# The third product of a finished block takes the identity and layer 2's root matrix along: rows of h and their root part from one product, in a two-layer relational graph network on one Trainium2 core

## The chip, the cores and the metric

The kernel runs on 1 core of one Trainium2 chip, as one program. The metric is the device time of one execution in microseconds (us). Before the change it is 3677.3 us, the median of 3 runs (3677.16, 3677.3 and 3686.43). Five engines run side by side and meet at semaphores: PE (matrix products; PEld is its loading of weights), DVE (vector operations), ACT (activations and copies), POOL (here it issues the gathers) and SP (it issues most of the other transfers).

## The reference

Two relational graph layers with a residual and a layer norm, over N = 12500 nodes, E = 200000 edges sorted by their target `dst`, C = 128 features and 10 relations; an edge's relation is the argmax of 10 of its 42 attributes.

```
def _rgcn_layer(x, src, dst, edge_type, w_rel, root, bias):
    N = x.shape[0]
    seg = dst * NUM_REL + edge_type
    xs = x[src]
    sums = jax.ops.segment_sum(xs, seg, num_segments=N * NUM_REL)
    cnt = jax.ops.segment_sum(jnp.ones(seg.shape, x.dtype), seg, num_segments=N * NUM_REL)
    mean = (sums / jnp.maximum(cnt, 1.0)[:, None]).reshape(N, NUM_REL, -1)
    return jnp.einsum('nrd,rdo->no', mean, w_rel) + x @ root + bias
...
edge_type = jnp.argmax(msg[:, NODE_EMB_DIM:-NODE_EMB_DIM], axis=1).astype(jnp.int32)
h = jax.nn.relu(_rgcn_layer(x, src, dst, edge_type, w_rel1, root1, b1))
return _rgcn_layer(h, src, dst, edge_type, w_rel2, root2, b2)
...
x = _layernorm(x + _L0_gnn_ref(...), axis=-1)
```

All of it is float32.

## The kernel before

**Tiles and blocks.** The edges lie in 1563 tiles of 128. Layer 1 walks over them in parts of `QB` = 4 tiles; this is the unit `u` of all times in the code, and `v` is half of it. For each tile POOL gathers the 128 source rows from memory (`gathered`, L835), DVE makes a matrix of weights by target (`oh`, L842), PE multiplies the two (`zp`, L1079), and two parts later DVE adds the result to `cc`, the sums by relation and node of a moving window (L868). PE, DVE, ACT, POOL and SP each work through their instructions in the order in which the program was written; a list `todo` of due times, in tiles, says behind which tile a step of other work is written.

The nodes lie in 52 blocks, most of them of 256 nodes (two halves of 128). Once the last edge of a block's nodes is summed, `finish(k, t)` writes the block's end into the stream of tiles:

- ten products of the sums with layer 1's weights and one of x's columns `fT` with root 1 (L828, L830) into PSUM, and the relu on ACT: `a`, the block's h as columns (L747). This is at once.
- Half a part later, for blocks 0 to `K1` = 43, `rows_out`: PE turns `a` into rows with two transposes (L953). Another half a part later, `rows_kept`: ACT copies them to `hb`, whose other half holds the rows of x (L960), and SP stores x and h side by side into `XH` (256 KB, L700). Later tiles whose source lies in a finished block gather these 256 columns: the x half serves layer 1, the h half layer 2's sums, so that an edge is gathered once for both layers.
- After one part, SP stores the block's layer-2 sums SD (1.28 MB, L803) and loads the next block's x.
- After two parts SP stores `a` to `hT` (128 KB, L965).
- After 2, 3, ... 7 parts, one step each of `projected_rows`: a 128-row half of h times layer 2's weights of relations 0 to 3, 4 to 7 (512 columns) and 8 to 9 (256 columns), into the one PSUM buffer `yb` (L936). Each step first writes the copy of the step before (`kept_rows`): ACT moves `yb` to one of two buffers `ys` (L942), and SP stores that to `YD` (L944). YD holds h times each relation's weights, and layer 2 gathers its rows for the edges whose source wasn't finished in time.
- After 5 and 6 parts the next block's x is turned on PE and copied by ACT (L998, L1005), and ACT clears parts of `cc` (L797).

**Layer 2** gathers from YD, with products `zy` and `zq` (L1620), sums on DVE into `acc2` (L1650), and for the SD sums products with layer 2's weights (L1533, L1540). A block's columns of `acc2` begin with `begun` (L1510, L1511): PE multiplies the loaded `hT` by root 2 into PSUM, and ACT adds the bias and writes `acc2`; three loads of `hT` are under way at a time. Its end turns `acc2` into rows on PE (L1552); DVE adds the rows of x, which are loaded for it, and norms them (L775 to L785).

In the trace's names `w` is a layer's weights, `root` its root matrix, `g` a gathered tile, `pf` a general PSUM tile with two buffers.

Of the kernel before, what the change touches and what calls it, by code (L numbers as in the profile page):

```python
# [9 lines left out]
F32 = mybir.dt.float32  # L10
# [10 lines left out]
P = 128  # L21
# [49 lines left out]
def rgcn_resnorm_kernel(ctx: ExitStack, tc: tile.TileContext, x, src, dst, attr, w_rel1, root1, b1,  # L71
# [152 lines left out]
    hT = dram.tile([C, N], F32, name="hT")  # L224
    XH = dram.tile([2 * N, 2 * C], F32, name="XH")
# [27 lines left out]
    ident = const.tile([P, P], F32, name="ident")  # L253
# [247 lines left out]
    def weights_in():  # L501
        for l, (wr, ro, bi) in enumerate(((w_rel1, root1, b1), (w_rel2, root2, b2))):
            t = const.tile([P, NREL, C], F32, name=f"w{l}")
            later(nc.sync.dma_start(t, wr.rearrange("r d o -> d r o")))
            wsb.append(t)
            t = const.tile([P, C], F32, name=f"root{l}")
# [198 lines left out]
    hbs = {}  # L705

    def rows_in(k):

        if home[0] is prep:
            if k == NBLK - 1:  # L710
                xb = fin.tile([P, 1, C], F32, name="xbe")
            else:
                hbs[k] = prep.tile([P, 2, 2 * C], F32, name=f"hb{k % 2}")
                xb = hbs[k][:, :, :C]
# [193 lines left out]
    def layer_1():  # L908
# [6 lines left out]
        def finish(k, t):  # L915
# [16 lines left out]
            def projected_rows(b, h, r):  # L932
                kept_rows()
                m = min(HB, NREL - r) * C
                yb = yb_ if u else next_of("zp", fixed)
                nc.tensor.matmul(yb[:h, :m], fin_a[k][:, b * P:b * P + h], wsb[1][:, r:r + m // C, :], start=True, stop=True)  # L936
                unkept.append(lambda: projected_kept(yb, b, h, r))

            def projected_kept(yb, b, h, r):
                ys = next_of("ys", staged)  # L940
                m = min(HB, NREL - r) * C
                nc.scalar.activation(ys[:h, :m], yb[:h, :m], AF.Copy)  # L942
                n0 = block(k)[0] + 1 + b * P
                nc.sync.dma_start(by_node[n0:n0 + h, r * C:r * C + m], ys[:h, :m])  # L944
# [3 lines left out]
            def rows_out(_):  # L948
                a = fin_a[k]
                pr = ps_f.tile([P, 4, C], F32, name="pf")  # L950
                n0, n, subs = block(k)
                for i, h in subs:
                    nc.tensor.transpose(pr[:h, i, :], a[:, i * P:i * P + h], ident)  # L953
                po.append(pr)

            def rows_kept(_):
                pr = po.pop()
                hb = hbs.pop(k)
                for p, s in spans(k):
                    nc.scalar.activation(hb[:p, s, C:], pr[:p, s], AF.Copy)  # L960
                rows_dma(hb, XH[N:], k, True)

            def features_kept(_):
                n0, n, _ = block(k)
                nc.sync.dma_start(hT[:, n0:n0 + n], fin_a[k][:, :n])  # L965

# [861 lines left out]
```

## Time and profile before

| what | value |
|---|---|
| median of 3 runs | 3677.3 us |
| the profiled execution, its time | 3672.03 us |
| the profiled execution, its span | 3670.2 us, 37654 instructions |
| mean granted TensorE clock | 0.753 |
| gathers of layer 1 from XH: x1386 | 1309.9 us of POOL, 945 ns each |
| gathers of layer 2's remaining edges, lists E and B: x177 and x678 | 168.2 and 640.3 us of POOL |
| projections of finished blocks, L936: x576 | 354.9 us of PE, 383.3 us idle before them |
| root products of layer 2, L1510: x102 | 39.2 us of PE, 65.3 us idle before them |

The table is read like this: "busy" is what an engine's instructions of a line took in all, "idle before" how long the engine stood just ahead of them, and the trace names what ended that. A 128-row product of float32 is recorded as two instructions. A tile of 128 edges is one gather.

### The profile page before, as it was taken

How to read it: one execution, taken by the hardware profiler on the slowest of the kernel's cores; microseconds unless marked ns; L12 is line 12 of the kernel's file. 1: busy time of each engine (PE TensorE's matmuls, PEld its weight loads, DVE VectorE, ACT ScalarE, POOL GpSimd, SP SyncE). 2: the span in 40 equal slices, each digit the busy share in tenths (PEclk: the TensorE clock that was granted, in tenths of full speed). 3: DMA queues.
4: the chain of work that ended last, by engine and by line, in shares of the span. 5: the costliest groups of instructions: out<-in, count | busy, mean ns of one | idle time of the engine just before them, and what ended most of it. 6: DMA issues, size and time to landing. Idle time of an engine off the chain costs nothing. (4 is left out here: it accounts for less than half of the span.)

```text
span 3670.2 us, 37654 instructions
## 1 busy us (share of the span) xinstructions
PE 2319.0 (63%) x10645; PEld 1779.5 (48%) x10645; DVE 1991.3 (54%) x6410; ACT 511.8 (14%) x799; POOL 2287.4 (62%) x2430
## 2 busy tenths in 40 slices
PE   1557676767676767677666767653566666566444
PEld 0445565555555555565555655543534343333333
DVE  4646476767575757565655656358644232332332
ACT  1111111212121212121212121110000000000000
POOL 5663666666666666666666666556666666666665
PEclk7677787888887888878888878765667777677555
DMA  4553555455555555555555555542334443443222
GB/s 121 159 164 94 187 157 186 151 167 159 177 174 159 189 158 190 158 192 159 190 156 188 159 159 156 147 111 55 105 112 139 129 153 123 148 152 116 61 57 52
DMA packets 345316, 529.25 MB, mean 144 GB/s; under 512 B 55520, under 2 KB 225723, under 8 KB 345100
## 3 DMA queue, kind: packets, MB, share of 16 engines
q0 software_dynamic: 99552, 249.45, 23.9%
q1 hardware_dynamic: 218105, 264.48, 21.7%
q10 hardware_dynamic: 27443, 12.82, 1.2%
q8 instruction: 89, 1.46, 0.2%
q14 instruction: 127, 1.04, 0.1%
HBM read 372.75 MB, written 160.19 MB: 145 GB/s over the span
## 5 line engine op out<-in xcount | busy, mean ns | idle before, releaser
L835 POOL DMA_INDIRECT g<-XH,idxE x1386 | 1309.9, 945 | 769.7 <-issue 368.6
L1079 PEld LDWEIGHTS zp<-oh,g 128*128 128x128 f32 x5898 | 918.4, 234 | 396.5 <-DVE cc L868 180.1
L1079 PE MATMUL zp<-oh,g 128*128 128x120 f32 x5898 | 957.0, 320 | 228.6 <-DVE cc L868 132.3
L868 DVE TENSOR_TENSOR cc<-cc,zp 128x240 f32 (+1 forms) x1563 | 606.5, 388 | 816.1 <-remote 354.1
L835 POOL DMA_INDIRECT g<-YD,idxB x678 | 640.3, 944 | 342.4 <-issue 190.7
L936 PE MATMUL yb<-w,a 128*128 128x512 f32 (+1 forms) x576 | 354.9, 706 | 383.3 <-ACT ys L942 229.0
L842 DVE TENSOR_SCALAR oh<-bank,keyE,wE 128x120 f32<-128x120 f32 x1563 | 517.3, 393 | 0.0
L1620 PEld LDWEIGHTS zy<-oh,g 128*128 128x128 f32 x1168 | 244.8, 275 | 317.9 <-DVE cc L1650 119.1
L1620 PE MATMUL zy<-oh,g 128*128 128x12 f32 (+30 forms) x1168 | 258.4, 347 | 206.5 <-DVE cc L1650 114.6
L942 ACT ACTIVATE ys<-yb 128x512 f32<-128x512 f32 (+2 forms) x291 | 152.8, 525 | 1384.8 <-remote 612.0
L1533 PE MATMUL alone<-cc,w 128*128 128x512 f32 (+1 forms) x440 | 305.3, 782 | 31.6 <-issue 16.9
L936 PEld LDWEIGHTS yb<-w,a 128*128 128x128 f32 x576 | 111.0, 240 | 413.7 <-ACT ys L942 255.9
L828 PE MATMUL pf<-cc,w 128*128 128x256 f32 (+2 forms) x1040 | 254.9, 401 | 25.7 <-issue 13.4
L835 POOL DMA_INDIRECT g<-in_x_dram,idxE x177 | 167.3, 945 | 138.2 <-PE zp L1079 60.0
L828 PEld LDWEIGHTS pf<-cc,w 128*128 128x128 f32 x1040 | 208.4, 215 | 63.9 <-issue 26.0
L835 POOL DMA_INDIRECT g<-YD,idxE x177 | 168.2, 951 | 110.8 <-issue 62.7
L775 DVE TENSOR_TENSOR cc<-pf,x 128x256 f32<-128x256 f32 (+2 forms) x52 | 21.2, 409 | 358.9 <-remote 219.9
L797 ACT ACTIVATE cc<-zero 128x1280 f32<-128x1280 f32 x170 | 214.6, 1262 | 0.0
L1620 PEld LDWEIGHTS zq<-oh,g 128*128 128x128 f32 x542 | 110.8, 253 | 151.2 <-DMA g<-YD,idxB 74.0
L842 DVE TENSOR_SCALAR oh<-columns,keyB,wB 128x45 f32<-128x45 f32 (+35 forms) x678 | 176.8, 335 | 0.0
L1620 PE MATMUL zq<-oh,g 128*128 128x45 f32 (+33 forms) x542 | 122.9, 341 | 84.3 <-DMA g<-YD,idxB 59.5
L1650 DVE TENSOR_TENSOR cc<-cc,zy 128x12 f32 (+24 forms) x306 | 59.0, 193 | 142.6 <-remote 61.0
(265 smaller groups left out, 1528.4 us busy)
## 6 DMA issues: line engine op xcount, KB each, us to landing
cc<-SD SPq DMA_DIRECT2D x21, 2560.0 KB
SD<-cc SPq DMA_DIRECT2D x41, 1280.0 KB
YD<-ys SPq DMA_DIRECT2D x194, 256.0 KB
m<-in_edge_attr_dram SPq DMA_DIRECT2D x48, 672.0 KB
g<-XH,idxE POOLq DMA_INDIRECT x1386
YD<-ys SPq DMA_DIRECT2D x97, 128.0 KB
XH<-hb SPq DMA_DIRECT2D x44, 256.0 KB
g<-YD,idxB POOLq DMA_INDIRECT x678
```

Source lines behind the costliest of these rows:

```text
L775: nc.vector.tensor_tensor(v[:p, s], pr[:p, s], xb[:p, s], op=ALU.add)
L797: nc.scalar.activation(cc[:, l, h * H:(h + 1) * H, o:o + n], zero[:, None, :n].to_broadcast([P, H, n]), AF.Copy)
L828: nc.tensor.matmul(po[:, :n], wsb[l][:, r, :], sums[:, r], start=(r == 0), stop=(w is None and r == NREL - 1))
L835: nc.gpsimd.indirect_dma_start(out=g[:, j * C:(j + n) * C], out_offset=None, in_=table, in_offset=bass.IndirectOffsetOnAxis(ap=idx, axis=0))
L842: nc.vector.tensor_scalar(oh[:, j * m:(j + 1) * m], cols[:, :m], keys[:, j:j + 1], weights[:, j:j + 1], op0=ALU.is_equal, op1=ALU.mult)
L868: nc.vector.tensor_tensor(s, s, z, op=ALU.add)
L936: nc.tensor.matmul(yb[:h, :m], fin_a[k][:, b * P:b * P + h], wsb[1][:, r:r + m // C, :], start=True, stop=True)
L942: nc.scalar.activation(ys[:h, :m], yb[:h, :m], AF.Copy)
L1079: nc.tensor.matmul(zp[:, o + l * KW:o + (l + 1) * KW], g[:, (slot[j] + l) * C:(slot[j] + l + 1) * C], oh[:, j * KW:(j + 1) * KW], start=Tr ...
L1533: nc.tensor.matmul(po[:, :n], wsb[1][:, r, :], sds[j][:, r, :n], start=(r == 0), stop=(r == NREL - 1))
L1620: nc.tensor.matmul(zp[:, o:o + w], g[:, at * C:(at + 1) * C], oh[:, j * w:(j + 1) * w], start=not second or j == 0, stop=not second or j = ...
L1650: nc.vector.tensor_tensor(s, s, zps[q][:, j * w:(j + 1) * w], op=ALU.add)
```

## The change

Layer 2's weights, its root matrix and the identity now lie side by side in one tile of 12 matrices, `w2`: relations 0 to 9, root, identity. The product of a half with "relations 8 and 9" is widened:

- For blocks 0 to 43 it takes 512 columns: relations 8 and 9, root, identity. It so gives the half's part of YD, the root part of layer 2, and the rows of h. It is now the first of a block's projections, for both halves at once (`rows_out`, half a part after the finish), one half into `yb`, the other into a `pf` tile. The transposes go. `rows_kept` copies both halves to the two `ys`; SP stores the rows of h to XH (64 KB a half) and the part of YD. The x half of XH is copied by SP from x in memory at the finish.
- One part later DVE adds the rows of x to the root part in `ys`, and SP stores that to a new array `XR` (`root_kept`, 64 KB a half). A `ys` buffer is taken again only when this is done.
- Four projections of 512 columns remain, after 2 to 5 parts.
- For blocks from 44 on the third product takes 384 columns (relations 8 and 9, root), and the root part goes to XR too.
- `hT` is neither stored nor loaded; `begun` only writes the bias to `acc2`; the end of layer 2 loads its rows from XR in place of x.

The core of the diff:

```
+    XR = dram.tile([N, C], F32, name="XR")
...
-    ident = const.tile([P, P], F32, name="ident")
+    w2 = const.tile([P, NREL + 2, C], F32, name="w1")
+    root = w2[:, NREL, :]
+    ident = w2[:, NREL + 1, :]
...
+            def projected_rows(t, b, h, r, yb=None):
+                if yb is None:
+                    kept_rows(t)
+                    yb = yb_ if u else next_of("zp", fixed)
+                m = width(r)
+                nc.tensor.matmul(yb[:h, :m], fin_a[k][:, b * P:b * P + h], w2[:, r:r + m // C, :], start=True, stop=True)
+                unkept.append(lambda t: projected_kept(t, yb, b, h, r))
+
+            def width(r):
+                return (HB if r + HB <= NREL or k <= K1 else NREL + 1 - r) * C
+
+            def projected_kept(t, yb, b, h, r):
+                if len(unrooted) == len(staged) or unrooted and unrooted[0][0] == turn_of_["ys"] - len(staged):
+                    unrooted.pop(0)[1]()
                 ys = next_of("ys", staged)
+                m = width(r)
                 nc.scalar.activation(ys[:h, :m], yb[:h, :m], AF.Copy)
+                n0 = block(k)[0] + b * P
+                q = min(HB, NREL - r) * C
+                if k <= K1 and m > q:
+                    nc.sync.dma_start(XH[N + n0:N + n0 + h, C:], ys[:h, q + C:q + 2 * C])
+                nc.sync.dma_start(by_node[n0 + 1:n0 + 1 + h, r * C:r * C + q], ys[:h, :q])
+                if m > q:
+                    one = turn_of_["ys"] - 1, lambda: root_kept(ys, n0, b, h, q)
+                    unrooted.append(one)
+                    todo.at(min(END, t + u), lambda _: one in unrooted and (unrooted.remove(one), one[1]()))
...
+            def root_kept(ys, n0, b, h, q):
+                nc.vector.tensor_tensor(ys[:h, q:q + C], ys[:h, q:q + C], xbs[k][:h, b, :], op=ALU.add)
+                nc.sync.dma_start(XR[n0:n0 + h, :], ys[:h, q:q + C])
+
+            def rows_out(t):
+                kept_rows(t)
+                for (b, h), yb in zip(block(k)[2], (yb_, ps_f.tile([P, YB], F32, name="pf"))):
+                    projected_rows(t, b, h, last, yb)
+
+            def rows_kept(t):
+                while unkept:
+                    unkept.pop(0)(t)
...
+            if k <= K1:
                 n0, n, _ = block(k)
-                nc.sync.dma_start(hT[:, n0:n0 + n], fin_a[k][:, :n])
+                nc.sync.dma_start(XH[N + n0:N + n0 + n, :C], x[n0:n0 + n, :])
...
         def begun(j):
-            po = ps_f.tile([P, YB], F32, name="pf")
-            nc.tensor.matmul(po[:, :n], rsb[1], fTs.pop(k)[:, :n], start=True, stop=True)
-            nc.scalar.activation(acc2[:, n0:n0 + n], po[:, :n], AF.Identity, bias=bsb[1])
-            features_in_turn(j + 3)
+            n0, n, _ = block(begin[j])
+            nc.scalar.activation(acc2[:, n0:n0 + n], zero[:, :n], AF.Identity, bias=bsb[1])
...
-                rows_dma(xbs[finals[j]], x, finals[j], False)
+                rows_dma(xbs[finals[j]], XR, finals[j], False)
```

PE, in layer 1, behind the finish of one block (the names: `zp` the products of edge tiles, `yb` and `pf` PSUM, `a` the block's h as columns, `w_391` layer 2's weights). Before:

```order
L1079 MATMUL zp_407<-oh_92,g_88 128x120 x2
L953 MATMUL pf<-ident,a 128x128 x2
L1079 MATMUL zp_408<-oh_92,g_88 128x120 x2
L1079 MATMUL zp_409<-oh_93,g_88 128x120 x2
L1079 MATMUL zp_410<-oh_93,g_88 128x120 x2
L936 MATMUL yb<-w_391,a 128x512
L1079 MATMUL zp_407<-oh_94,g_89 128x120 x2
L1079 MATMUL zp_408<-oh_94,g_89 128x120 x2
L936 MATMUL yb<-w_391,a 128x512
L1079 MATMUL zp_409<-oh_95,g_89 128x120 x2
L297 MATMUL pf<-ident,s_f 128x128
L1079 MATMUL zp_410<-oh_95,g_89 128x120 x2
```

And the same block in the changed kernel (`w_114` is the tile of 12 matrices, so that the last row, a small turn of edge data with the identity, names it too):

```order
L1087 MATMUL zp_406<-oh_93,g_89 128x120 x2
L937 MATMUL yb<-w_114,a 128x512
L937 MATMUL pf<-w_114,a 128x512
L1087 MATMUL zp_407<-oh_93,g_89 128x120 x2
L1087 MATMUL zp_408<-oh_94,g_89 128x120 x2
L1087 MATMUL zp_409<-oh_94,g_89 128x120 x2
L937 MATMUL yb<-w_114,a 128x512
L1087 MATMUL zp_406<-oh_95,g_90 128x120 x2
L1087 MATMUL zp_407<-oh_95,g_90 128x120 x2
L937 MATMUL yb<-w_114,a 128x512
L1087 MATMUL zp_408<-oh_96,g_90 128x120 x2
L300 MATMUL pf<-w_114,s_f 128x128
```

The two transposes have become two products of 512 columns, the second of them into `pf`; the next projection stands where the first stood before, and the 256-column one behind the second of 512 is gone: the fourth 512-column projection now stands one step earlier.

SP, for one block in the middle of layer 1, with what each row waits for beside being next in line (a DMAHW semaphore is one of eight that SP's transfers use in turn). Before, all ten transfers of a block:

```order
L700 DMA XH<-hb_7834 128x2x256 [waits DMAHW1_49,Activation_49]
L803 DMA SD<-cc 1280x1x256 [waits DMAHW2_49]
L700 DMA hb_8190<-in_x_dram 128x2x128 [waits DMAHW3_49,PE_49]
L965 DMA hT<-a 128x256 [waits DMAHW4_49]
L944 DMA YD<-ys_99 128x512 [waits DMAHW5_49,Activation_49]
L944 DMA YD<-ys_100 128x512 [waits Activation_49]
L944 DMA YD<-ys_99 128x256 [waits DMAHW7_49,Activation_49]
L944 DMA YD<-ys_100 128x512 [waits DMAHW0_49,Activation_49]
L944 DMA YD<-ys_99 128x512 [waits DMAHW1_49,Activation_49]
L944 DMA YD<-ys_100 128x256 [waits DMAHW2_49,Activation_49]
```

After, the first twelve of the thirteen transfers of a block (the last, another store to YD, is left out):

```order
L978 DMA XH<-in_x_dram 256x128 [waits DMAHW3_49]
L952 DMA XH<-ys_100 128x128 [waits DMAHW4_49,Activation_49]
L953 DMA YD<-ys_100 128x256 [waits DMAHW5_49]
L952 DMA XH<-ys_101 128x128 [waits DMAHW6_49,Activation_49]
L953 DMA YD<-ys_101 128x256 [waits DMAHW7_49]
L803 DMA SD<-cc 1280x1x256 [waits DMAHW0_49,DVE_49]
L703 DMA xb_8564<-in_x_dram 128x2x128 [waits DMAHW1_49,PE_49]
L963 DMA XR<-ys_100 128x128 [waits DMAHW2_49,DVE_49]
L963 DMA XR<-ys_101 128x128 [waits DMAHW3_49,DVE_49]
L953 DMA YD<-ys_100 128x512 [waits DMAHW4_49,Activation_49]
L953 DMA YD<-ys_101 128x512 [waits DMAHW5_49,Activation_49]
L953 DMA YD<-ys_100 128x512 [waits DMAHW6_49,Activation_49]
```

The one store of x and h has become a copy of x at the front and two stores of h's rows, each with a store to YD behind it; the store of `hT` is gone; the two XR stores stand behind the store of the sums and the load of the next x, and ahead of the first of the four remaining stores to YD.

PE, at one place in layer 2 (`alone` are the products of the stored sums, `zy` those of gathered edges). Before:

```order
L1533 MATMUL alone<-cc,w_391 128x512
L1620 MATMUL zy_15679<-oh_93,g_86 128x85 x2
L1533 MATMUL alone<-cc,w_391 128x512
L1384 MATMUL pf<-ident,keyb 38x1
L1510 MATMUL pf<-cc,root_393 128x256 x2
L1620 MATMUL zy_15680<-oh_94,g_86 128x89
L1533 MATMUL alone<-cc,w_391 128x512
L1620 MATMUL zy_15680<-oh_94,g_86 128x89 x2
```

After:

```order
L1529 MATMUL alone<-cc,w_114 128x512
L1614 MATMUL zy_15778<-oh_94,g_87 128x85 x2
L1529 MATMUL alone<-cc,w_114 128x512
L1392 MATMUL pf<-w_114,keyb 38x1
L1614 MATMUL zy_15779<-oh_95,g_87 128x89
L1529 MATMUL alone<-cc,w_114 128x512
L1614 MATMUL zy_15779<-oh_95,g_87 128x89 x2
L1529 MATMUL alone<-cc,w_114 128x512
```

The pair of root products is gone from between the edge products, and nothing stands in its place.

More of the change, by code (lines that the diff above doesn't have):

```diff
@@ L704, in rgcn_resnorm_kernel @@
     home = [prep]
-    hbs = {}
     def rows_in(k):
@@ L964, in features_kept @@
+            last = NREL // HB * HB
+            groups = [(b, h, r) for b, h in block(k)[2] for r in range(0, NREL, HB) if k > K1 or r < last]
+            if k <= K1:
                 n0, n, _ = block(k)
-                nc.sync.dma_start(hT[:, n0:n0 + n], fin_a[k][:, :n])
-            groups = [(b, h, r) for b, h in block(k)[2] for r in range(0, NREL, HB)]
-            if k <= K1:
+                nc.sync.dma_start(XH[N + n0:N + n0 + n, :C], x[n0:n0 + n, :])
                 todo.at(t + v, rows_out)
@@ L1558, in layer_2 @@
             nc.sync.dma_start(rowP[:, c * CT:(c + 1) * CT], b_i[c:c + 1, :])
-        for j in range(3):
-            features_in_turn(j)
         for j in range(3):
```

56 lines of the change are left out of this document (10 added, 46 removed).

## The prediction

> **What bounds the kernel now.** I read the page's totals first, then two long stretches of the busy-time windows, then the waits and the groups by shape inside the first of them.
>
> ```profile
> span 3670.2 us, 37654 instructions
> PE 2319.0 (63%) x10645; PEld 1779.5 (48%) x10645; DVE 1991.3 (54%) x6410; ACT 511.8 (14%) x799; POOL 2287.4 (62%) x2430
> ...
> core 0: us, PE busy (x) PEld busy (x) DVE busy (x) ACT busy (x) POOL busy (x), PEclk, DMA share, GB/s
> 500.00:2300.00 1800.00, 1259.57 (x6514) 1021.22 (x6512) 1142.80 (x3369) 361.67 (x497) 1143.15 (x1210) 0.82 0.54 169
> 2700.00:3450.00 750.00, 467.99 (x1643) 292.86 (x1641) 251.60 (x1090) 26.25 (x72) 489.91 (x519) 0.73 0.42 133
> ```
>
> No engine is full anywhere. The first stretch is the steady part of layer 1; it holds 38 finished blocks (38 stores of the sums, and 152 copies of 512 columns at four a block), so a block takes 1800/38 = 47.4 us. The second is the late part of layer 2. POOL issues gathers of 0.945 us, and between two that wait for nothing stand 0.30 us (the timeline below: 1533.34, 1534.59, 1535.84). So its own pitch is 1.25 us, and 1210 gathers would need 1512 of the 1800 us; 288 us, or 7.6 us a block, are POOL standing. In layer 2, 519 gathers need 649 of 750 us, and about 101 us are standing.
>
> What POOL stands for in layer 1 is PE, which frees the gathered tiles late, and what PE stands for is this:
>
> ```profile
> POOL g L835 <- issue: 323.0, 1051, 0.8
> POOL g L835 <- remote: 170.6, 81, 3.1
> POOL g L835 <- PE zp L1079: 136.0, 58, 7.6
> POOL g L835 <- DMA XH<-hb: 0.6, 2, 0.3
> ...
> PE yb L936 <- ACT ys L942: 184.7, 57, 8.6
> PE yb L936 <- issue: 97.6, 32, 7.9
> ...
> L936 PE MATMUL yb<-w,a 128*128 128x512 f32 x304 | 221.4, 819 | 245.9 <-ACT ys L942 142.9 <-issue 73.1 <-DMA g<-XH,idxE 29.9
> L936 PE MATMUL yb<-w,a 128*128 128x256 f32 x152 | 61.3, 491 | 66.7 <-ACT ys L942 41.9 <-issue 24.5
> L953 PE MATMUL pf<-ident,a 128*128 128x128 f32 x72 | 16.9, 321 | 43.4 <-ACT a L747 34.7 <-DMA g<-XH,idxE 8.0 <-issue 0.7
> ```
>
> The reader sees one dominant wait on PE: a projection step (L936) into the single buffer `yb` waits until ACT has copied the step before it to `ys`. The two L936 rows carry 245.9 + 66.7 = 312.6 us of idle, 8.2 us a block over six steps. This is close to the 7.6 us that POOL stands, so I take layer 1 as a loop limited by PE with its waits for ACT, with POOL little behind. PE waits for gathered data little (29.9 + 8.0 us in 38 blocks): it has a stock of gathers.
>
> One passage of the timeline shows such a wait:
>
> ```profile
> 1530.74 0.38 ACT L960 ACTIVATE hb<-pf 128x256 f32<-128x256 f32 x1 [1.84 <-PE zp L1079]
> 1531.15 0.37 SPq L700 DMA_DIRECT2D XH<-hb  x1
> 1531.61 0.52 SPq L803 DMA_DIRECT2D SD<-cc  x1
> 1532.49 1.03 PE L936 MATMUL yb<-w,a 128*128 128x512 f32 x2
> 1533.34 0.95 POOL L835 DMA_INDIRECT g<-XH,idxE  x1 [0.30 <-issue]
> 1534.59 0.95 POOL L835 DMA_INDIRECT g<-XH,idxE  x1 [0.30 <-issue]
> 1535.84 0.95 POOL L835 DMA_INDIRECT g<-XH,idxE  x1 [0.30 <-issue]
> 1541.16 0.60 ACT L942 ACTIVATE ys<-yb 128x512 f32<-128x512 f32 x1 [8.88 <-issue]
> 1541.81 1.22 PE L936 MATMUL yb<-w,a 128*128 128x512 f32 x1 [6.15 <-ACT ys L942]
> ...
> q1 hardware_dynamic: 1584, 1.58, 86.7%
> ```
>
> The first `yb` is done at 1533.5, its copy starts only at 1541.16, and PE stands 6.15 us. Between them lies the 1.28 MB store SD; in the six microseconds from 1532 on, SP's queue q1 moved 1.58 MB, so SD alone takes about 1.31/1.58 x 6 = 5.0 us (an estimate from that row).
>
> **The change, part by part, layer 1.** 44 blocks (0 to 43) take the new form.
>
> 1. Two 256-column steps a block go, with their waits. Busy 61.3/38 = 1.61 us, idle 66.7/38 = 1.76 us: -3.37 us. The steps left are the four 512-column ones, and I keep their waits as they are.
> 2. The transposes of L953 go: 16.9 us for 36 recorded blocks, -0.47 us. The wait ahead of them (43.4 us) is for the relu `a`; the new products stand at the same place and inherit it. It isn't saved.
> 3. Two 512-column products come at that place. A 128-row product is two instructions; 304 in 221.4 us make 1.46 us for each product: +2.91 us.
> 4. The first of the four steps used to find `yb` free; now it must wait for the copy of the third product. Ends: 0, and 245.9/152 = 1.62 us, the mean idle before a 512-column step. The copies are queued one unit of four tiles ahead of that step, so I take 0.2, near the lower end. Behind a PE that waits there stand the products of the next tiles, and behind them DVE's sums.
> 5. `ys` has two buffers, and each is now held until DVE has added x and SP has stored XR. The next copy into it waits for that, and `yb` with it. Ends: 0, and again 1.62 us a buffer (3.24 us a block). I take 0.2: the next copy stood 9.55 us after SD's issue in the passage above, and SD needs about 5.0.
> 6. ACT: four copies of 0.597, two of 0.381 and one of 0.383 us become six of 0.597: 3.53 to 3.58 us. Nothing.
>
> ```profile
> L942 ACT ACTIVATE ys<-yb 128x512 f32<-128x512 f32 x152 | 90.7, 597 | 857.3 <-issue 383.7 <-remote 306.6 <-PE zp L1079 129.8
> L942 ACT ACTIVATE ys<-yb 128x256 f32<-128x256 f32 x75 | 28.6, 381 | 246.4 <-remote 191.2 <-PE yb L936 44.0 <-issue 6.1
> L960 ACT ACTIVATE hb<-pf 128x256 f32<-128x256 f32 x36 | 13.8, 383 | 34.7 <-PE pf L953 20.9 <-PE zp L1079 13.8
> L583 DVE TENSOR_TENSOR bad<-bad,far 128x128 f32<-128x128 f32 x8 | 2.3, 292 | 0.3
> ```
>
> 7. DVE: two 128x128 adds; the nearest row, L583, gives 0.292 us: 0.58 us a block. DVE is busy 1142.80 of 1800 us, which hides it; without that cover, +26 us in all.
> 8. SP issues 13 transfers a block in place of 10 (two XH stores, two XR and the copy of x come; the one XH store and the hT store go). At 0.37 to 0.52 us each (rows above) that is 1.1 to 1.6 us of SP in 47 us, which SP has. What stands behind the XR stores on SP is the first YD store, which itself waits for a copy one unit later. In bytes: XH and hT (384 KB) become h, x and XR (384 KB); nothing, or, if the extra read of x counts, 0.5 us a block at q1's rate, +22 us.
> 9. The rows of h leave later: the products cost 2.4 us more than the transposes, and one copy more stands ahead of the second store (2 x 0.60 - 0.38 = 0.8): 3.3 us. The gathers that need them wait today for almost nothing (0.6 us in all). Ends: 0 and 3.3 us of POOL a block. I take 0, because PE works off a stock of gathers, and it comes later itself.
>
> Sum a block: -3.37 - 0.47 + 2.91 + 0.2 + 0.2 = **-0.53 us, x 44 = -23 us**. The last eight blocks (two of 256 nodes, six shorter: ten halves) widen a 256-column step to 384, half of (1.46 - 0.81) each, 0.81 being 61.3/76: **+3 us**.
>
> **Layer 2.** `begun` loses its product with the root matrix, the load of hT, and the PSUM tile; the ACT instruction stays, and waits for nothing on PE.
>
> ```profile
> L1510 PE MATMUL pf<-cc,root 128*128 128x256 f32 (+2 forms) x102 | 39.2, 486 | 65.3 <-issue 38.9 <-DVE cc L775 14.7 <-ACT cc L1511 11.7
> L1552 PE MATMUL pf<-ident,cc 128*128 128x128 f32 x98 | 31.6, 380 | 113.8 <-DVE cc L1650 37.4 <-issue 36.8 <-ACT cc L1511 22.7
> ...
> 2926.94 0.59 PE L1510 MATMUL pf<-cc,root 128*128 128x256 f32 x2
> 2938.90 1.22 PE L1510 MATMUL pf<-cc,root 128*128 128x256 f32 x2 [11.36 <-DVE cc L775]
> ...
> POOL g L835 <- issue: 253.1, 768, 8.3
> POOL g L835 <- remote: 102.7, 32, 4.6
> POOL g L835 <- PE zy L1620: 54.2, 23, 8.0
> POOL g L835 <- PE zq L1620: 14.8, 7, 4.1
> ```
>
> PE loses 39.2 us of work and the 11.7 + 22.7 us it stood for L1511: 73.6 us at most. How much reaches the end is what POOL feels. From 2400 us on, these four rows sum to 424.8 us; PE is named in 69.0 (16%), and with `remote`, which may hide PE, in 171.7 (40%). I take 30%, between: **-22 us**; ends 0 and -74. What is late next there is the DVE sum ahead of the transposes (L1552 <- L1650, 37.4 us). The x rows of the end now come from XR by the same loads: nothing.
>
> Total: -23 + 3 - 22 = -42. The profiled execution took 3672.0 us (span 3670.2 and 1.8 us around it), so **3630 us**. The median shown, 3677.3, lies 5.3 us (0.14%) higher; on that scale the same sum gives 3635.
>
> **The rivals.** *A larger gain.* If each step that goes takes a sixth of all the idle with it (2.73 us in place of 1.76), and nothing new is waited for, a block gains 2.73 + 1.61 + 0.47 - 2.91 = 1.9 us: -84. Then the clock: after the wait of 6.15 us a single 512-column instruction took 1.22 us, where two took 1.03 just before; the granted clock is 0.82. From 0.82 to 0.85, PE's 1259.57 us in the stretch shrink by 44 us, 51 over 44 blocks; half of that reaching the end is -26. With half of layer 2's 74: 3672 - 84 - 26 - 37 + 3 = 3528. Against it: the waits come mostly with the large store, and the store stays. The Trainium skill, "TensorE: Matmul & The Clock Gate", section "HAM oscillation — how this bites in real kernels", says that PE idle beyond about 3.4 us brings the clock down for the work behind it; the two rows of 0.5 and 1.22 us agree, and by that rule alone two gaps fewer would pay as priced here.
>
> *Hidden.* POOL's pitch or SD sets the block, and PE merely waits elsewhere: within 0.3%, some 3665 to 3680. For it: POOL's own pitch covers 1512 of 1800 us.
>
> *Slower.* One mechanism: the XR stores queue behind SD. They are issued some 6 us after it, on the same queue, and hold both `ys` buffers; the first copy of the block waits for them, PE for the copy, the next tiles' products for PE. With 1.62 us for each buffer the block becomes 3.24 - 0.93 = 2.3 us longer (0.93 is the sum without waits): 3672 + 102 + 3 - 22 = 3755; with 2.4 us in all, 3718. It decides once the new waits exceed 0.93 + 19/44 = 1.4 us a block. For it: SP's queue held 86.7% of the DMA engines there. Against it: 9.55 us between SD's issue and the copy. The Trainium skill, "DMA: Bandwidth & Descriptors", section "Queues, rings and completion order", says that each DMA engine takes the descriptors of one ring in order; by that rule a 64 KB store issued behind SD would land only after it. No row of this case shows two such stores side by side.
>
> That the change wouldn't do what it says I rule out: the rows of the changed program stand as described.
>
> **How the numbers follow.** Forecast (3590 to 3660): 0.47. Larger gain (3500 to 3590): 0.18. Hidden: 0.17. Slower (3690 to 3760): 0.18. A measurement of this kernel can tell about 0.3%, 11 us, from no change. So faster 0.65, same 0.17, slower 0.18. The range goes from 3545, which takes in half of the larger gain, to 3700, which takes in the lightest slower cases; it leaves out some 0.09 below and 0.11 above. The ends of items 4, 5 and 9 taken together would lie above it; they are unlikely to fall together.
>
> **What would show it.** In the 500 to 2300 stretch: 304 instructions of the 512-column shape become about 456, with idle before the whole group near 245 us; above 310 item 4 or 5 is wrong. ACT's copies waiting for `XR<-ys` would be the slower rival. POOL waiting for `XH<-ys` by more than 1 us a block would prove item 9 wrong. More than 38.5 blocks in 1800 us, a gather pitch under 1.45 us there (1.488 now), and layer 2 shorter by 10 to 40 us are the forecast; a granted clock of 0.85 or more there is the larger gain. The order of PE's waits staying at 8 us a block although two steps are gone would make the prediction wrong towards "hidden".

## The result and the profile after

The changed kernel takes **3722.9 us** (median of 4 runs, 3709.5 to 3724.4) against 3677.2 us for the kernel before, measured beside it: the ratio is **1.0116, 95% interval 1.0100 to 1.0132**. It is slower by 46 us, where 3630 us and a gain were forecast; the range (3545 to 3700) doesn't hold it.

The profiled execution took 3724.35 us, 52.3 us more than that of the kernel before. First the page's totals, then the same windows, groups and waits as before the change.

```profile
span 3722.6 us, 37538 instructions
PE 2326.5 (62%) x10455; PEld 1727.6 (46%) x10455; DVE 2012.8 (54%) x6508; ACT 512.6 (14%) x755; POOL 2288.4 (61%) x2430
```

The windows of busy time, 500 to 2300 us:

```profile
500.00:2300.00 1800.00, 1257.26 (x6265) 971.04 (x6266) 1136.17 (x3380) 355.64 (x450) 1115.10 (x1180) 0.82 0.54 165
```

The granted clock of the stretch is 0.82, as before. In the same 1800 us there are 1180 gathers in place of 1210. At POOL's own pitch of 1.25 us they need 1475 us, so POOL stands 325 us, and with 37 finished blocks that is 8.8 us a block against 7.6 before. A block takes 48.9 us in place of 47.7 (from the starts of the finishes). 44 blocks at 1.2 us make 53 us: the loss lies in layer 1. Layer 2's first gather starts here:

```profile
2447.11 0.94 POOL L835 DMA_INDIRECT g<-YD,idxE  x1 [10.58 <-PE zp L1087]
```

Before, the same row stands at 2397.14. So 50.0 us are lost by then, and layer 2 gains nothing.

The groups by shape in the 500 to 2300 stretch (L937 is the projection, L948 its copy, L962 the addition of x):

```profile
L937 PE MATMUL yb<-w,a 128*128 128x512 f32 x368 | 272.0, 830 | 366.5 <-issue 148.2 <-ACT ys L948 135.5 <-ACT a L747 71.1
L937 PE MATMUL pf<-w,a 128*128 128x512 f32 x72 | 55.1, 861 | 0.0
L948 ACT ACTIVATE ys<-yb 128x512 f32<-128x512 f32 x184 | 109.8, 597 | 759.3 <-remote 260.4 <-DMA XR<-ys 143.7 <-issue 127.0
L962 DVE TENSOR_TENSOR ys<-ys,xb 128x128 f32<-128x128 f32 x72 | 20.2, 291 | 83.9 <-ACT ys L948 53.4 <-issue 30.5
```

Two steps a block are gone, but the idle time ahead of the projections isn't: 366.5 us in 37 blocks, 9.9 us each, where the steps and the transposes had 312.6 + 43.4 in 38, 9.4 each. And ACT's copies wait for XR stores (143.7 us), as the slower rival said.

The waits of POOL in the same stretch:

```profile
POOL g L835 <- issue: 311.2, 1018, 0.9
POOL g L835 <- remote: 163.3, 70, 3.0
POOL g L835 <- PE zp L1087: 105.9, 49, 8.9
POOL g L835 <- PE yb L937: 19.0, 6, 5.7
POOL g L835 <- DMA XH<-ys: 18.5, 5, 4.8
```

The last of these rows is small, but it stood at 0.6 us before. It names only a part: a wait is put down to the releaser that came last by the profile. One block's timeline shows it better:

```profile
1510.05 0.59 PE L830 MATMUL pf<-fT,root 128*128 128x256 f32 x2
1517.79 0.47 ACT L747 ACTIVATE a<-pf,b 128x256 f32<-128x256 f32 x1 [19.71 <-remote]
1518.31 2.08 PE L937 MATMUL yb<-w,a 128*128 128x512 f32 x2 [5.88 <-ACT a L747]
1520.18 1.92 PE L937 MATMUL pf<-w,a 128*128 128x512 f32 x2
1521.05 0.32 SPq L952 DMA_DIRECT2D XH<-ys  x1
1522.80 0.32 SPq L952 DMA_DIRECT2D XH<-ys  x1
...
1526.30 0.94 POOL L835 DMA_INDIRECT g<-XH,idxE  x1 [3.23 <-PE zp L1087]
```

The gather at 1526.30 is the first that reads this block's rows of h. It starts 3.50 us after the second store of the rows was issued, and POOL stood 3.23 us ahead of it. In the passage shown in the prediction the gather with the same place is the one at 1535.84: 4.69 us after the store at 1531.15, with nothing but its own issue (0.30 us) ahead. Over 34 blocks, with the landing read from the transfers' semaphores (the last update on record), this gather starts 0.76 to 0.91 us (10th to 90th percentile) after the second store has landed; before, 1.00 to 2.55 us after. A spread that small says that it waits for the landing in nearly every block. POOL stands 2.76 us ahead of it in the mean, against 0.36; of the 36 blocks of the stretch, it stands more than 0.5 us there in all, before the change in 5.

### The profile page after: what moved, and what is told of

Same layout as the page of the kernel before. It is cut to its first block, busy times and chain, and to the rows that moved or that the text cites. A ratio compares the mean times of both kernels' runs of the same rounds, so it can differ in the third digit from the quotient of the medians.

```text
span 3722.6 us, 37538 instructions
## 1 busy us (share of the span) xinstructions
PE 2326.5 (62%) x10455; PEld 1727.6 (46%) x10455; DVE 2012.8 (54%) x6508; ACT 512.6 (14%) x755; POOL 2288.4 (61%) x2430
## 5 line engine op out<-in xcount | busy, mean ns | idle before, releaser
L1087 PEld LDWEIGHTS zp<-oh,g 128*128 128x128 f32 x5898 | 869.6, 225 | 424.2 <-DVE cc L868 217.6
L1087 PE MATMUL zp<-oh,g 128*128 128x120 f32 x5898 | 909.2, 312 | 241.5 <-DVE cc L868 163.0
L937 PE MATMUL yb<-w,a 128*128 128x512 f32 (+1 forms) x488 | 354.1, 816 | 465.0 <-issue 187.9
L937 PEld LDWEIGHTS yb<-w,a 128*128 128x128 f32 x488 | 94.1, 241 | 494.7 <-issue 217.0
L828 PE MATMUL pf<-cc,w 128*128 128x256 f32 (+2 forms) x1040 | 272.3, 419 | 37.2 <-issue 23.0
L948 ACT ACTIVATE ys<-yb 128x512 f32<-128x512 f32 (+2 forms) x247 | 146.4, 593 | 1002.4 <-remote 347.9
L828 PEld LDWEIGHTS pf<-cc,w 128*128 128x128 f32 x1040 | 217.2, 225 | 84.2 <-issue 43.2
L781 ACT ACTIVATE rstd<-mv,eps 128x2 f32<-128x2 f32 (+2 forms) x52 | 15.3, 295 | 1109.4 <-DVE mv L779 706.3
```

The lines of the kernel that those rows point to most:

```text
L781: nc.scalar.activation(rstd[:p, s], mv[:p, s, 1], AF.Sqrt, bias=eps[:p])
L828: nc.tensor.matmul(po[:, :n], wsb[l][:, r, :], sums[:, r], start=(r == 0), stop=(w is None and r == NREL - 1))
L1087: nc.tensor.matmul(zp[:, o + l * KW:o + (l + 1) * KW], g[:, (slot[j] + l) * C:(slot[j] + l + 1) * C], oh[:, j * KW:(j + 1) * KW], start=Tr ...
```

## The experiments

The runs took place on chips of two kinds: on one the kernel before takes 3636 to 3677 us, as in the result above, on the other 3095 to 3098. What the change costs is made up differently on the two, so the table says for each run how long the kernel before takes on its chip; each ratio is to the kernel before on the same chip. In the names, READY is the number of parts between a block's finish and the first gather that reads its rows of h (5 in both kernels), "spread" means that the four remaining projections stand after 2, 3.5, 5 and 6.5 parts in place of 2, 3, 4 and 5, and "rows late" that the rows of h are made and stored half a part later.

| run | what | kernel before there | ratio (95% interval) |
|---|---|---|---|
| result | the changed kernel | 3677 | 1.0116 (1.0100 to 1.0132) |
| e1 | changed, without XR | 3675 | 1.0121 (1.0094 to 1.0148) |
| e2 | identity alone | 3675 | 1.0126 (1.0107 to 1.0146) |
| e3 | root part alone | 3675 | 1.0007 (0.9993 to 1.0021) |
| e4 | layer 2's part alone | 3675 | 0.9972 (0.9959 to 0.9985) |
| e13 | changed, without XR, spread | 3636 | 1.0108 (1.0072 to 1.0144) |
| e14 | changed, without XR, READY 6 | 3636 | 1.0014 (1.0003 to 1.0025) |
| e15 | kernel before, 256-column product early | 3636 | 1.0044 (1.0026 to 1.0062) |
| e9 | the changed kernel | 3098 | 1.0148 (1.0117 to 1.0179) |
| e10 | changed, spread | 3098 | 1.0063 (1.0042 to 1.0083) |
| e5, e11, e17 | changed, READY 6 | 3095 to 3098 | 1.0112, 1.0121, 1.0123 |
| e8 | changed, READY 6, spread | 3095 | 1.0032 (1.0019 to 1.0045) |
| e18 | changed, READY 6, tiles of its own for XR | 3095 | 1.0097 (1.0083 to 1.0111) |
| e12 | kernel before, 256-column product early | 3098 | 1.0040 (1.0026 to 1.0055) |
| e6 | kernel before, READY 6 | 3095 | 1.0009 (0.9999 to 1.0018) |
| e7, e16 | kernel before, rows late | 3095, 3098 | 0.9998, 0.9996 |

**Which part loses: e1 to e4** (slower kind).

e1 leaves the addition and XR out:

```
-                    unrooted.append(one)
-                    todo.at(min(END, t + u), lambda _: one in unrooted and (unrooted.remove(one), one[1]()))
...
-                rows_dma(xbs[finals[j]], XR, finals[j], False)
+                rows_dma(xbs[finals[j]], x, finals[j], False)
```

> The changed kernel without root_kept: DVE adds nothing to the root part, SP stores no XR, and the end of layer 2 loads x, so that layer 2's root part is left out of the output. The third product, its copies and the stores of h's rows are unchanged. Theory 1 (the XR stores hold the two ys buffers behind the 1.28 MB store of the sums; ACT's copy waits 143.7 us for them in the stretch from 500 to 2300): the copies start early again and nearly all of the 46 us come back, 3670 to 3685. Theory 2 (the third product at its early place is what costs: PE stands 121 us ahead of it in that stretch where it stood 43 ahead of the transposes, and h's rows leave 6 us later): little comes back, 3705 to 3722.

Measured 1.0121. No part of the loss came back; theory 1 falls for this kind of chip. Its trace agrees with theory 3 below: POOL stands 2.48 us ahead of the first gather of the new rows (mean of 36 blocks from 500 to 2300; 0.41 before, 2.73 in the changed kernel).

e2 keeps the identity and drops the root part. Beside the lines below, hT, its loads and the product of begun are put back as they were:

```
-    root = w2[:, NREL, :]
-    ident = w2[:, NREL + 1, :]
+    root = w2[:, NREL + 1, :]
+    ident = w2[:, NREL, :]
...
-                return (HB if r + HB <= NREL or k <= K1 else NREL + 1 - r) * C
+                return (HB if r + HB <= NREL else NREL - r + (k <= K1)) * C
```

> One part of the change alone: the third product takes relations 8 and 9 and the identity (384 columns) at its early place and gives h's rows; the root part stays in layer 2 as before (hT stored and loaded, product at begun), there is no XR. Theory 1 (XR): about the time of before or a little less, 3655 to 3680, since the two 256-column steps are gone and no buffer is held. Theory 2 (the early third product): most of the loss is here, 3705 to 3725.

Measured 1.0126: by its time, the whole loss is here. In its one profile layer 2's first gather stands 29.5 us later than before, and the other 12 us of that execution lie in layer 2, whose program is that of the kernel before; so one profile leaves open how the loss divides.

e3 is the reverse; the old `rows_out`, `rows_kept` and `hb` are put back, and

```
-                return (HB if r + HB <= NREL or k <= K1 else NREL + 1 - r) * C
+                return (HB if r + HB <= NREL else NREL + 1 - r) * C
...
-            groups = [(b, h, r) for b, h in block(k)[2] for r in range(0, NREL, HB) if k > K1 or r < last]
+            groups = [(b, h, r) for b, h in block(k)[2] for r in range(0, NREL, HB)]
```

> The other part alone: transposes, hb and the one store of x and h as before, six projection steps as before, of which the third and sixth take 384 columns (8, 9, root); x added, XR stored, layer 2 begins with the bias alone. Theory 1 (XR holds ys): slower than before, 3700 or more, with ACT waiting for XR. Theory 2 (the early third product): 3670 to 3685, since XR is stored here when no store of the sums is under way.

Measured 1.0007, and ACT hardly waits for XR (9.0 us from 500 to 2300, against 143.7). The root part costs nothing where it doesn't stand ahead of the store of the sums. It brings nothing either.

e4 takes only layer 2's part, into the kernel before:

```
-            todo.at(t + 2 * u, features_kept)
...
-            po = ps_f.tile([P, YB], F32, name="pf")
-            nc.tensor.matmul(po[:, :n], rsb[1], fTs.pop(k)[:, :n], start=True, stop=True)
-            nc.scalar.activation(acc2[:, n0:n0 + n], po[:, :n], AF.Identity, bias=bsb[1])
-            features_in_turn(j + 3)
+            nc.scalar.activation(acc2[:, n0:n0 + n], zero[:, :n], AF.Identity, bias=bsb[1])
```

> The kernel before with layer 2's part of the change alone: begun writes the bias without the product with root 2, hT is neither stored nor loaded, the root part is left out of the output. As predicted (-22 us in layer 2, nothing in layer 1): 3650 to 3660. As the profile after reads, where the gathers of layer 2 take 1257 us from first to last against 1251 before: no gain, 3672 to 3684.

Measured 0.9972, 10 us (5 to 15): between the two. In its one profile the first gather of layer 2 stands 7.8 us earlier than before, and layer 2 from first to last gather takes 1249.1 us against 1251.1. So what there is of a gain seems to come from the store of hT that goes, in layer 1, and not from the product; one profile of each kernel doesn't settle that.

**What of the early product loses, on the slower kind: e13 to e15.** These were meant to tell three theories apart: that the rows of h come late (3), that the copies are packed into the first five parts of a block (4), that the width costs (5).

e14 moves the first use of the rows by one part (and leaves XR out, as e1):

```
-READY = 5
+READY = 6
```

> The changed kernel without root_kept and XR (layer 2's root part is left out of the output) and with READY 6. On a chip of the slower kind (XR left out alone: 1.0121): theory 3 (late rows of h stop POOL, 2.5 us a block) 0.998 to 1.005; theory 4 (packing) 1.010 or more. On one of the faster kind (READY 6 alone: 1.0121 and 1.0112): theory 1 (XR holds ys behind the store of the sums: ACT waits 216 us for it there from 500 to 2000) 1.000 to 1.005; otherwise 1.009 or more.

Measured 1.0014, where e1 had 1.0121 on another chip of this kind and e13 (below), with READY 5, has 1.0108 on the same chip: nearly all is back. Its timeline, at the store of one block's rows and the first gather that reads them, now a part later:

```profile
1529.47 0.36 SPq L952 DMA_DIRECT2D XH<-ys  x1
...
1537.48 0.94 POOL L835 DMA_INDIRECT g<-XH,idxE  x1 [1.21 <-remote]
```

8.01 us lie between the two, against 3.50 in the changed kernel; in the 22 blocks whose landing the trace holds the gather starts 3.7 to 6.6 us after it (10th to 90th percentile). At its old place, four tiles earlier, POOL now stands 0.55 us in the mean, and 1.41 at the new one, where the kernel before stands 0.98 on the other chip. The window of 500 to 2300:

```profile
500.00:2300.00 1800.00, 1277.97 (x6469) 998.78 (x6470) 1148.89 (x3391) 366.25 (x466) 1149.18 (x1216) 0.82 0.55 168
```

1216 gathers, where e13 on the same chip has 1193, with the early wide products all there. So theory 2, that those products at their early place are what costs, falls too. (The 1210 gathers of the kernel before were counted on the other, slower chip.)

e13 spreads the four remaining projections (and leaves XR out):

```
-                i = 2 + j if k <= K1 else 1 + j
-                todo.at(t + i * u, lambda t, b=b, h=h, r=r: projected_rows(t, b, h, r))
+                i = (2 + 3 * j / 2) if k <= K1 else 1 + j
+                todo.at(t + int(i * u), lambda t, b=b, h=h, r=r: projected_rows(t, b, h, r))
```

> The changed kernel without root_kept and XR (layer 2's root part is left out of the output) and with its four remaining projections after 2, 3.5, 5 and 6.5 parts. On a chip of the slower kind, where leaving out XR alone gave 1.0121 times the kernel before: theory 4 (packing) 1.002 to 1.007, theory 3 (late rows) or theory 5 (the wide early product) 1.010 or more. On one of the faster kind, where spreading alone gave 1.0063: if XR's hold on ys still counts there, 0.998 to 1.003; if not, 1.004 to 1.008.

Measured 1.0108, against 1.0121 without the spreading: nothing that can be told apart. PE's wait ahead of the projections went to other places, and POOL still stood 2.64 us ahead of the first gather of the new rows (36 blocks). Theory 4 falls here.

e15 changes the kernel before in one place; transposes, hb and the store of the rows stay ahead of the products:

```
                 po.append(pr)
+                kept_rows()
+                for (b, h), yb in zip(subs, (yb_, ps_f.tile([P, YB], F32, name="pf"))):
+                    projected_rows(b, h, last, yb)
...
                 rows_dma(hb, XH[N:], k, True)
+                while unkept:
+                    unkept.pop(0)()
```

> The kernel before with the third product of both halves (256 columns) at the early place and nothing else, again: it gave 1.0040 on a chip of the faster kind. On one of the slower kind theory 4 (place and packing) gives 1.007 to 1.014, theory 5 (the width, and the rows of h behind it) 0.997 to 1.004; on the faster kind, 1.003 to 1.006 as before.

Measured 1.0044 (1.0026 to 1.0062), just above what theory 5 allowed and under what theory 4 asked for. Here the rows wait only for what the two products add ahead of them, and POOL stands 0.90 us ahead of the gather (36 blocks): in size between the kernel before (0.41; 1.000) and the changed one (2.73; 1.0116). Theory 3 orders the three.

**The same on the faster kind: e5 to e12 and e16 to e18.**

> The changed kernel with READY 6 in place of 5: the first gather that reads a finished block's rows of h stands one part (four tiles) later. In the changed kernel that gather starts 0.76 to 0.91 us after the second XH store lands in nearly every block, and POOL stands 2.76 us ahead of it in the mean, against 0.36 us before the change. Theory 3 (the rows of h come late, and POOL waits for them): the standing ahead of that gather falls under 0.6 us, and the time comes back to 3665 to 3690. Theory 2 (PE standing ahead of the early third product is what costs): nothing comes back, 3710 to 3725.

> Control: the kernel before with READY 6. Its gathers hardly wait for h's rows (0.36 us ahead of the first one of a block, issue included), so by theory 3 nothing is gained; a few more edges are left to layer 2's own gathers, so it costs some: 3675 to 3692. If it is faster than before by more than 10 us, READY 5 was already too early.

> The kernel before with one edit: rows_out and rows_kept (transposes, copy to hb, store to XH) each half a part later; no product is added, moved or widened. Theory 3: the gather that needs the rows now waits for them in most blocks, and the time rises to 3695 to 3725. Theory 2: the transposes find the relu done and stand less, 3665 to 3680.

 Its edit:

```
-                todo.at(t + v, rows_out)
-                todo.at(t + 2 * v, rows_kept)
+                todo.at(t + 2 * v, rows_out)
+                todo.at(t + 3 * v, rows_kept)
```

> The changed kernel with READY 6 and the four projections that remain spread over the block, after 2, 3.5, 5 and 6.5 parts in place of 2, 3, 4 and 5. If the packing of the steps costs (PE stands about 3 us ahead of every second step, waiting for the copy of the step before): 15 to 35 us under the kernel with READY 6 alone. If PE's idle time only follows what POOL and the late signals set (it was 14.2 to 15.5 us a block in all kernels so far): within 6 us of it.

Measured 1.0112, 1.0009, 0.9998 and 1.0032. On this kind rows that leave half a part later still landed 2.2 us and more before their gather in three blocks of four (e7), and POOL stood 0.3 us a block for them: late rows alone cost next to nothing here. Instead the spreading paid 0.8%. The changed kernel itself, the spreading alone, READY 6 again and the early product follow:

> The changed kernel itself, as a control beside the next three: the runs with READY 6 took place on a chip on which the kernel before needs 3095 us in place of 3675, and there the changed kernel was not run. Expected: 1.010 to 1.013 times the kernel before, on either kind of chip.

> The changed kernel (READY 5) with its four remaining projections after 2, 3.5, 5 and 6.5 parts in place of 2, 3, 4 and 5. Theory 4 (the change packs a block's six copies PE to ACT to PE into its first five parts, and PE waits there): about 0.8% better than the changed kernel, as with READY 6, so 1.003 to 1.006 times the kernel before. Theory 3 (late rows of h): unchanged, 1.010 to 1.013.

> The changed kernel with READY 6, again, beside the changed kernel itself. On a chip of the slower kind theory 3 (late rows) gives 1.000 to 1.004 times the kernel before, theory 4 (packing) 1.009 to 1.013, with POOL standing elsewhere for as long. On one of the faster kind, where the gather found its rows 3 to 13 us early, both give 1.010 to 1.013.

> The kernel before with one edit: the third product of both halves (relations 8 and 9, 256 columns, as before) moves to the early place behind the transposes, one half into yb, the other into pf; four 512-column projections remain after 2 to 5 parts. No identity, no root, no XR; transposes, hb and the one store of the rows stand ahead of it as before. Theory 4 (place and packing cost): most of the loss is here, 1.007 to 1.013 times the kernel before. Theory 5 (the width: 512 columns ahead of the rows of h, and two copies of 512 columns): 0.997 to 1.003.

Measured 1.0148, 1.0063, 1.0121 and 1.0040. In e9 the slower rival of the prediction is plain, waits of ACT and PE from 500 to 2000 us:

```profile
ACT ys L948 <- PE yb L937: 312.0, 147, 9.2
ACT ys L948 <- DMA XR<-ys: 216.2, 26, 9.9
...
PE yb L937 <- ACT ys L948: 57.4, 21, 6.0
```

and in e10, spread, two of the three are smaller:

```profile
ACT ys L948 <- DMA XR<-ys: 121.0, 17, 9.7
PE yb L937 <- ACT ys L948: 11.0, 8, 3.1
```

> The kernel before with rows_out and rows_kept half a part later and nothing else, again: on a chip of the faster kind it gave 0.9998 times the kernel before, with h's rows landing 2.4 us and more before the gather that reads them in three blocks of four. On one of the slower kind, where that gather has 1.8 us to spare in the median, theory 3 (late rows stop POOL) gives 1.005 to 1.012, with POOL standing about 2 us ahead of that gather in the mean; if the loss of the changed kernel lies elsewhere, 0.998 to 1.003.

> The complete changed kernel with READY 6, a third time: on chips of the faster kind it gave 1.0112 and 1.0121. On one of the slower kind, where READY 6 brought the version without XR from 1.0121 to 1.0014, theory 3 gives 1.000 to 1.005; if XR's hold on ys then shows, 1.005 to 1.010.

> The complete changed kernel with READY 6 and with two tiles of its own for the sum of x and the root part, so that a ys buffer is free once DVE has added, whatever becomes of the XR store. On a chip of the faster kind (READY 6 alone: 1.0112, 1.0121 and 1.0123): if XR's hold on ys is what is left there, 1.000 to 1.006; if not, 1.009 or more. On one of the slower kind (READY 6 without XR: 1.0014): 1.000 to 1.005 by theory 3; more if the add itself, in line on DVE, costs.

e16 and e17 repeat e7 and e5 on the faster kind: 0.9996, 1.0123. e18 writes the sum to tiles of its own:

```
-                nc.vector.tensor_tensor(ys[:h, q:q + C], ys[:h, q:q + C], xbs[k][:h, b, :], op=ALU.add)
-                nc.sync.dma_start(XR[n0:n0 + h, :], ys[:h, q:q + C])
+                xr = next_of("xr", rooted)
+                nc.vector.tensor_tensor(xr[:h, :], ys[:h, q:q + C], xbs[k][:h, b, :], op=ALU.add)
+                nc.sync.dma_start(XR[n0:n0 + h, :], xr[:h, :])
```

Measured 1.0097 (1.0083 to 1.0111). PE no longer waits for copies there (1.4 us in 1500), and yet only some 0.15 to 0.26 points come back, less than e5's interval on the same chip is wide. So XR's hold costs little on this kind, and that it costs anything isn't shown. READY 6 and the spreading together take the ratio from 1.0148 to 1.0032 (e9 and e8, on two chips); 0.4 points for the early place (e12) can't be added to that, as e12 packs the steps too.

Where it is lost can be read from POOL. A block's 32 gathers at 1.25 us need 40.0 us, and on this kind a block takes 40.1 us in e6 and 41.1 in e9: the gathers set the pace, and what POOL stands is paid in full. Over 34 blocks it stands, beyond its own issue, 0.2 us a block in e6, 1.2 in e9, 0.6 in e10, 0.7 to 0.9 with READY 6 (e5, e11, e17) and 0.3 with both (e8). Of e9's 1.2 us, 0.5 stands ahead of the first gather of the new rows, in 10 of the 34 blocks; so, by these profiles, late rows are a part of the loss here too. Why packed steps cost POOL time when PE doesn't wait for the copies is not settled.

No version that gives the reference's whole output beat the kernel before on either kind of chip (e1, e4, e13 and e14 leave layer 2's root part out).

## Why the prediction was wrong

**Item 9 is the step that failed.** It said that the rows of h leave 3.3 us later, gave 0 and 3.3 us of POOL a block as ends, and took 0, "because PE works off a stock of gathers, and it comes later itself". The runs put it near the other end: POOL stands 2.4 us a block longer ahead of the first gather of the new rows (2.76 against 0.36), and moving that gather back by one part takes the ratio of the version without XR from 1.0121 (e1; e13, on e14's chip, 1.0108) to 1.0014. By name POOL waits only 0.5 us a block for `XH<-ys`, under the 1 us that the prediction set as the sign; the rest stands under other names. The stock of gathers doesn't cover it, since POOL's own pitch fills 40 of 47.7 us: what POOL loses at one place it can win back only from its other waits. It did so for half: 1.2 us a block remain of 2.4, and the profiled layer 1 is 50 us longer. Those 50 us and the 42 of gain that did not come are nearly all of the 94 between the forecast's 3630 and the profiled execution. The profile of before held the warning: of 3.92 us between the issue of the store and the gather (median), some 2.2 are the transfer, so the rows had under 2 us to spare, against a delay that the prediction itself put at 3.3.

**Item 2 made the delay larger, though not the loss.** The new products were to inherit the transposes' wait for the relu. That wait grew: PE's idle named `ACT a` went from 34.7 to 71.1 us, and the last store of the rows is issued 16.8 us after the start of the finish in place of 10.5 (medians): 6.4 us later, not 3.3. The relu itself comes 4.77 us after the product it waits for, 2.83 before (means from 500 to 2300). What makes it later is open; in e14 it is 3.14. But in e1 it is 2.95, near that of before: there the last store leaves 4.0 us later than before in the mean (14.5 us after the start of the finish against 10.5), not much more than item 9's 3.3, and the loss is the same. So a delay of about that size was enough for the loss.

**Item 1 saved nothing on this kind of chip.** PE's busy time came as worked out (+0.93 us a block by the groups, +0.83 forecast: (272.0 + 55.1)/37 against (221.4 + 61.3)/38 + 16.9/36), but the 1.76 us of idle didn't go with the steps. In every kernel run on the slower kind PE stands 13.7 to 15.5 us a block in all, whatever steps are removed, spread or moved. That is how the rival "hidden" reads it: a remainder of a pace set elsewhere, so that the wait that PE names is not a cost that can be taken off. The reading "a loop limited by PE" did not hold; what sets the pace on this kind beside POOL's 40 us of own pitch is not shown.

**Items 4 and 5.** The first of the four steps did not wait (0.02 us a block, 0.2 taken). The 366.5 us of idle ahead of the 512-column group are over the 310 that were to prove item 4 or 5 wrong, yet 71.1 of them are the relu's. XR's hold appeared as the slower rival had it, 143.7 us of ACT standing; that rival's price was refuted here, since e1 without XR is as slow. The XR stores are issued 2.1 and 3.4 us behind SD (medians), not some 6, and land 1.0 us after it in the median; 2 of 58 land before it, by up to 0.4 us. The Trainium skill, "DMA: Bandwidth & Descriptors", section "Queues, rings and completion order", says that each DMA engine takes one ring's descriptors in order; the trace agrees in the main, by these landings.

**Items 3, 6, 7 and 8** held: the 512-column products into `yb` take 1.48 us each by the same group and those into `pf` 1.53 (1.46 taken), the copies 0.597, the addition 0.291 us (0.292), and e3, which has the additions and the XR stores, shows that they and SP's part in them cost nothing.

**Layer 2**, -22 us in the forecast: the changed kernel shows none of it (1257 us from first to last gather, 1251 before), and e4 measured 10 us (5 to 15) for all of that part, hT's store included. That PE doesn't set the pace there either, so that its 39.2 us of products cost little, fits this and was not tested by itself.

**The larger gain** needed a granted clock of 0.85 or more in the stretch; it stayed at 0.82.

What isn't shown: READY 6 in the complete changed kernel, and in the kernel before, on a chip of the slower kind; both ran on the faster only. What READY 6 alone could give the kernel before there is bounded by its trace: of the 0.36 us ahead of that gather 0.30 are the issue, so 0.06 x 44 = 3 us.

## What to carry to other kernels

Ask of a change that delays a result who reads it first, and how much time that reader has to spare today; a wait that reads as nothing in the profile may be 2 us away from being paid in every round. Where an engine's own pitch fills most of a round (40 of 47.7 us here), a stall of it is only partly won back, while idle time of a less loaded engine reappears wherever its waits are removed: subtract the wait of a step only if that engine sets the pace. Undoing one half of the change at a time (e2, e3) found the losing half in a single comparison.

## What the runs showed of the hardware that was not expected

The same kernel takes 3675 us on some chips and 3095 us on others (medians of 18 and 22 runs); the granted clock was about 0.75 in those runs and about 0.80 in these. The traces differ in when PE's results become known. On the faster kind the relu starts 0.04 us after the recorded end of the product it waits for, in the median and at the 90th percentile (e6); on the slower kind 2.8 us after it in the median before the change and 6.5 after, up to 8 us (blocks from 500 to 2300). In the block shown in the section on the result the product ends at 1510.64; the semaphore that PE raises rises three times within 0.2 us from 1517.76 on, and the relu starts at 1517.79, while PE stands from 1512.43 to 1518.31. Throughout that stretch the relu starts 0.02 us after the last recorded rise. Of that semaphore's recorded updates from 500 to 1900 us, 40% follow another within 0.2 us in the kernel before, and under 1% in e6. The recorded ends of products are modelled, so the traces don't tell whether the product or its signal is late. The projections of e6 wait 5.7 us in the whole run:

```profile
L936 PE MATMUL yb<-w,a 128*128 128x512 f32 (+1 forms) x576 | 310.9, 627 | 5.7 <-ACT ys L942 5.0 <-DMA g<-in_x_dram,idxE 0.6
```

The same group of the kernel before on the slower kind has 383.3 us of idle. So nearly all the waits ahead of the projections, on which the prediction's layer 1 was built, show on that kind of chip only. What delays PE's signals there was not found.
